# A perceiver block on one core: an attention product computed in the first step, layer norms beside the batches, a rearranged last batch

## The chip, the core and the metric

The kernel runs on one core of a Trainium2 chip. The core has TensorE (PE; its weight loads are shown as PEld), VectorE (DVE), ScalarE (ACT), GpSimd (POOL) and SyncE (SP), each with its own queue of instructions that it works through in order. DMAs are issued by SP, ACT and POOL. The metric is the device time of one execution in microseconds (us), the median over several executions. One execution is also profiled; its span runs from the first to the last instruction.

## What is computed

Eight batches of 128 rows with 512 columns go through three residual blocks. Normalisation is over the columns.

```python
x = x + xattn(layernorm(x), ctx)   # 8 heads of 64, softmax over 2048 context rows
x = x + attn(layernorm(x))         # n = layernorm(x); adds n + read
#   queries = n@Wq+bq, keys = n@Wk+bk, values = n@Wv+bv; causal mask;
#   probs = softmax(logits, axis=1) / sqrt(512), read = probs @ values
x = x + ffn(layernorm(x))
#   h = relu(n@w1.T + b1); rounded to a float of 4 exponent and 3 mantissa bits,
#   as is w2; out = h@w2.T + b2, rounded to 5 exponent and 10 mantissa bits
```

The context has 2048 rows of 384 columns in each batch, so its keys and values (`pk`, `pv`) are most of the work.

## The kernel before

**Cross-attention.** The loop over batches `b` has four steps `m`, one for each pair of heads. A step issues `scores(b, m)` (TensorE `sc`; VectorE copies each bank to `p` and takes maxima, L530), then `attend` of the pair before (TensorE `po`, L571), then one *unit* of other TensorE work, and around it `exps` for the two heads (ScalarE, L544), `turns` (VectorE transposes `p` in 32 by 32 blocks, L557, and SP issues 16 DMAs that put the blocks into `pT`, L560). `pT` and `p` have one buffer each. The unit is `v_proj(b, 1)`, `v_proj(b+1, 0)` or `k_proj(b+1, m-2)`: products of blocks of the context in a scheme with 20 products instead of 24, whose operands are sums of context blocks (`sum_half`, on POOL except for batch 0) and of weight blocks (`sum_w`). A unit is a generator: its first part runs between the two `exps` (`first_of`), the rest after `turns` (`all_of`).

**Order.** Under `manual_schedule` an engine keeps the order of the program text; otherwise a scheduler orders its instructions. TensorE keeps the text's order to the end. ScalarE (`in_turn`) and VectorE (`first`) keep it until these two contexts are closed, in the last batch at the end of step 0. POOL and SP are always left to the scheduler. All queues are worked off in order on the chip.

**Start.** Before the loop, batch 0 is prepared: `k_plain`, the queries of all batches (`q_norm`, `q_turn`, `q_proj`; normed rows of the second half in the buffer `v0`), `sum_half` of both halves on VectorE, `keep_rows` (POOL adds the output bias `bo` to all rows, L503, and SP stores them to `xd`), and preparation for the self-attention. There, logits are computed as n (Wk Wq^T) n^T with side terms: `weight_by_bias` multiplies each weight by a bias row (`dot`, L303), `turn_weight` transposes both weights in blocks on VectorE (L313), and `keep_weights` stores them by 32 DMAs (L320) in DRAM.

**Rows.** `normalized_first` and `normalized` (in step 0 of the next batch) divide by the softmax sums, `project` (L609, L612) adds the output projection to the rows of the batch before, and SP stores these to `xr` (L614). `bring_rows` loads all rows back in the last batch.

**Last batch, self-attention, ffn.** In step 0 of batch 7 `enter_self_attention` closes the pools of the context and loads weights through POOL's queue. `SelfAttention` 0 has rows 0 to 3, 1 has rows 4 to 7. The last batch's units are, in step 1, `both_weights` (product of the two weights, `psw`, L664) followed by `norm` and `turn` of rows 0 to 3; in step 2 `keys` (`psk`, L678); in step 3 `weights` of four rows (`pl`, L693, mask, softmax). Then come the `values` (`psv`, L717), `attend` of the last pair, `project` of batch 7, norms and turns of rows 4 to 7, the second half of the self-attention, `read` (`pr`, L725), and the ffn: `hidden` (`ph`, L927; ScalarE's relu, L931; `quantize`, five VectorE instructions, L40 to L44), `output` (`pf`, L936) and `finish`.

Of the kernel before, what the change touches and what calls it, by code (L numbers as in the profile page):

```python
# [23 lines left out]
E4M3 = (3, -6, 8)  # L24
# [3 lines left out]
def quantize(nc, pool, out, x, fmt, tag):  # L28
# [15 lines left out]
    nc.vector.tensor_scalar(out, r, 2.0 ** (128 - over), 2.0 ** (over - 128), ALU.mult, ALU.mult)  # L44


@with_exitstack
def tile_perceiver_block(
# [226 lines left out]
    bo = tmp.tile([P, D], F32, tag="t", name="bo")  # L275
    nc.sync.dma_start(bo, xa_bo.partition_broadcast(P))
# [3 lines left out]
    side = const.tile([P, 2, NK], F32, tag="side", name="side")  # L280
    both_biases = const.tile([P, 1], F32, tag="both_biases", name="both_biases")
    turned_w = [dram.tile([D, D], F32, tag=f"tw{i}", name=f"tw_{i}") for i in range(2)]

    def across(v, n, name):

        line = dram.tile([1, D], F32, tag=f"line{n}", name=f"line_{n}")
        nc.gpsimd.dma_start(line.rearrange("o (k p) -> p (o k)", p=P), v)
        return line[0].partition_broadcast(P)

    for i, a in enumerate((sa_wq, sa_wk)):  # L290
        nc.sync.dma_start(w_sa[:, i], a.rearrange("(k p) n -> p k n", p=P))
    bias_rows = []
    for n, a in (("bk", sa_bk), ("bq", sa_bq)):
        c = const.tile([P, NK], F32, tag=f"c{n}", name=f"c_{n}")
        nc.gpsimd.dma_start(c, a)
        t = tmp.tile([P, D], F32, tag="t", name=f"row_{n}")
        nc.gpsimd.dma_start(t, across(c, n, n))
        bias_rows.append(t)

    unread = ps_acc.tile([P, D], F32, tag="po", name="unread")  # L300

    def dot(to, one, two):
        nc.vector.scalar_tensor_tensor(unread, one, 1.0, two, ALU.mult, ALU.mult, accum_out=to)  # L303

    def weight_by_bias(i):

        for k in range(NK):
            dot(side[:, i, k : k + 1], w_sa[:, i, k], bias_rows[i])

    def turn_weight(i, ks):  # L310

        for k in ks:
            nc.vector.transpose(w_sa[:, i, k], w_sa[:, i, k])  # L313

    def keep_weights():
        for i in range(2):
            for k in range(NK):
                for a in range(Q):
                    to = turned_w[i][:, k * P + a * SQ : k * P + (a + 1) * SQ]
                    nc.sync.dma_start(  # L320
                        to.rearrange("(g i) j -> i g j", i=SQ),
                        w_sa[ts(a, SQ), i, k].rearrange("p (g j) -> p g j", j=SQ),
                    )
# [177 lines left out]
    def keep_rows(g):  # L501
        for b in range(g * GB, (g + 1) * GB):
            nc.gpsimd.tensor_tensor(xs[b], xs[b], bo, ALU.add)  # L503
        nc.sync.dma_start(xd[:, ts(g, GB), :], x_in[:, ts(g, GB), :])
# [96 lines left out]

    def load_x(b):
        xs[b] = xp.tile([P, D], F32, tag="x", name=f"x_{b}")
        nc.sync.dma_start(xs[b], xd[:, b, :])

    def project(b, ot):
# [6 lines left out]
        if b < B - 2:  # L613
            nc.sync.dma_start(xr[:, b, :], xs[b])  # L614

    def bring_rows():
        t = keep.tile([P, B, D], F32, tag="keep", name="rows")
        nc.gpsimd.dma_start(t[:, : B - 2], xr[:, : B - 2])
        nc.gpsimd.dma_start(t[:, B - 2 :], xd[:, B - 2 :])
        for r in range(B):  # L620
            xs[r] = t[:, r, :]


    def load_row(pool, src, name):
        t = pool.tile([P, D], F32, tag=name, name=name)
        nc.gpsimd.dma_start(t, src.partition_broadcast(P))
# [7 lines left out]
    class SelfAttention:  # L634


        def __init__(self, g, pool, w):
            self.g, self.pool = g, pool
            self.swq, self.swk, self.swv, self.u, self.bv, self.mask = w
            self.c = {}  # L640
# [17 lines left out]
        def both_weights(self):  # L658

            self.both = self.pool.tile([P, NK, D], F32, tag="sq", name="both")  # L660
            for m in range(NK):
# [7 lines left out]
                if m == 1:  # L669
                    yield  # L670
# [358 lines left out]
```

## Time and profile before

| | |
|---|---|
| median of 3 executions | 1127.91 us (1126.43 to 1130.67) |
| profiled execution | 1124.47 us, span 1122.7 us |
| granted TensorE clock, mean | 0.992 |
| TensorE busy in the span | 1098.4 us (98%) |
| VectorE, ScalarE, POOL busy | 844.1, 334.7, 236.1 us (75%, 30%, 21%) |
| one of the batches 1 to 6 | 102.86 us (scores at 227.97, 330.84, ...) |
| scores of batch 7 to the first `ph` | 157.84 us (816.72 to 974.56) |
| first `ph` to the end of the chain's last piece of `ph` | 126.1 us (974.56 to 1100.65) |
| from there to the end | 22 us |

A matrix product of float32 is recorded as two matmul entries. TensorE's busy time is modelled from pipelined entries, so 98% does not mean that it runs at its peak. A name such as `pv_z` is a tile of the program with its buffer number left out. In the pieces of the chain the columns are start and duration in us, then engine, tile, line and number of instructions. In the stretches in order of time they are start, duration, engine, line, operation, tiles and shapes, number, and in brackets the idle time of the engine just before, with what ended it.

### The profile page before, as it was taken

How to read it: one execution, taken by the hardware profiler on the slowest of the kernel's cores; microseconds unless marked ns; L12 is line 12 of the kernel's file. 1: busy time of each engine (PE TensorE's matmuls, PEld its weight loads, DVE VectorE, ACT ScalarE, POOL GpSimd, SP SyncE). 2: the span in 40 equal slices, each digit the busy share in tenths (PEclk: the TensorE clock that was granted, in tenths of full speed). 3: DMA queues.
4: the chain of work that ended last, by engine and by line, in shares of the span. 5: the costliest groups of instructions: out<-in, count | busy, mean ns of one | idle time of the engine just before them, and what ended most of it. 6: DMA issues, size and time to landing. Idle time of an engine off the chain costs nothing.

```text
span 1122.7 us, 16820 instructions
## 1 busy us (share of the span) xinstructions
PE 1098.4 (98%) x6254; PEld 830.2 (74%) x6254; DVE 844.1 (75%) x1760; ACT 334.7 (30%) x527; POOL 236.1 (21%) x328
## 2 busy tenths in 40 slices
PE   9989999999999999999999999999998999999997
PEld 4467788877878887888778788878874564687775
DVE  3988767767867786677777667866787468997777
ACT  3323232222223332322222233323232323232221
POOL 1401610440053045004400530350002100000001
PEclk9989999999999999999999999999998999999999
DMA  8858544553553355445535533554474445200001
GB/s 213 279 129 135 129 99 111 146 151 76 142 143 83 85 148 146 101 109 146 150 76 142 141 76 85 148 137 92 108 209 120 108 95 225 75 1 20 10 10 38
DMA packets 66785, 130.10 MB, mean 116 GB/s; under 512 B 27456, under 2 KB 32592, under 8 KB 65808
## 3 DMA queue, kind: packets, MB, share of 16 engines
q1 hardware_dynamic: 64144, 121.68, 43.6%
q0 software_dynamic: 1696, 6.57, 2.0%
q8 instruction: 49, 0.80, 0.3%
q10 hardware_dynamic: 864, 0.79, 0.2%
q14 instruction: 32, 0.26, 0.1%
HBM read 51.92 MB, written 9.97 MB: 55 GB/s over the span
## 4 chain that ended last, share of the span: by engine, by line
PE 88%; DVE 7%; DMA 3%; issue 1%; ACT 0%; SPq 0%; ACTq 0%; DVEq 0%
PE pv_z L450 20%; PE pk_z L427 19%; PE po L571 11%; PE sc L526 10%; PE ph L927 9%; PE pv_b L450 3%; PE pk_b L427 3%; PE psk L678 2%; PE psv L717 2%; PE py L609 2%; PE pf L936 2%; DMA x<-in_ctx_t_dram 1%; PE psw L664 1%; DVE m L205 1%; DMA x_in<-in_x_dram 1%; DVE x L205 1%
## 5 line engine op out<-in xcount | busy, mean ns | idle before, releaser
L544 ACT ACTIVATE p<-p,nm 128x2048 f32<-128x2048 f32 x64 | 128.2, 2003 | 429.4 <-DVE nm L538 291.2
L557 DVE STREAM_TRANSPOSE p<-p 128x512 f32<-128x512 f32 x256 | 158.9, 680 | 82.8 <-ACT p L544 82.6
L530 DVE TENSOR_SCALAR_CACHE_REDUCE p<-sc 128x512 f32<-128x512 f32 x256 | 159.0, 686 | 21.0 <-PE sc L526 18.6
L450 PE MATMUL pv_z<-wv_sums,x 128*128 128x256 f32 x640 | 158.0, 381 | 1.8 <-DVE v L353 1.8
L427 PE MATMUL pk_z<-x,wk_sums 128*128 128x256 f32 x600 | 151.0, 385 | 5.5 <-DVE kt L353 4.9
L205 POOL TENSOR_TENSOR m<-x 128x256 f32<-128x256 f32 x70 | 51.1, 731 | 485.4 <-DMA x<-in_ctx_t_dram 388.9
L450 PEld LDWEIGHTS pv_z<-wv_sums,x 128*128 128x128 f32 x640 | 120.4, 190 | 20.3 <-DVE v L353 2.2
L427 PEld LDWEIGHTS pk_z<-x,wk_sums 128*128 128x128 f32 x600 | 113.4, 191 | 25.1 <-DVE kt L353 5.6
L571 PEld LDWEIGHTS po<-pT,v 128*64 128x64 f32 x2048 | 112.4, 138 | 25.0 <-issue 23.5
L526 PE MATMUL sc<-kt,q 64*128 64x512 f32 x512 | 120.9, 604 | 3.8 <-DVE p L530 2.5
L571 PE MATMUL po<-pT,v 128*64 128x128 f32 x2048 | 120.2, 276 | 0.0
L927 PE MATMUL ph<-xf,w 128*128 128x256 f32 x512 | 111.3, 379 | 0.0
L450 PE MATMUL pv_z<-wv_sums,m 128*128 128x256 f32 x448 | 107.5, 380 | 0.2 <-ACT v L347 0.2
L927 PEld LDWEIGHTS ph<-xf,w 128*128 128x128 f32 x512 | 97.2, 190 | 13.9 <-issue 0.5
L427 PE MATMUL pk_z<-m,wk_sums 128*128 128x256 f32 x420 | 102.0, 381 | 0.0
L526 PEld LDWEIGHTS sc<-kt,q 64*128 64x128 f32 x512 | 47.6, 187 | 63.7 <-issue 52.7
L450 PEld LDWEIGHTS pv_z<-wv_sums,m 128*128 128x128 f32 x448 | 83.3, 190 | 13.3 <-issue 0.9
L427 PEld LDWEIGHTS pk_z<-m,wk_sums 128*128 128x128 f32 x420 | 79.8, 191 | 11.7
L347 ACT COPY v<-pv_z 128x512 f32<-128x512 f32 x112 | 62.8, 588 | 59.8 <-PE pv_z L450 59.6
L347 ACT COPY kt<-pk_z 128x512 f32<-128x512 f32 (+1 forms) x112 | 59.7, 558 | 63.1 <-PE pk_z L427 62.7
L205 POOL TENSOR_TENSOR x<-x 128x256 f32<-128x256 f32 x98 | 69.9, 730 | 0.8 <-DMA x<-in_ctx_t_dram 0.7
L350 DVE TENSOR_TENSOR v<-pv_z,v 128x512 f32<-128x512 f32 x96 | 63.2, 686 | 5.1 <-PE pv_z L450 5.0
(187 smaller groups left out, 1233.1 us busy)
## 6 DMA issues: line engine op xcount, KB each, us to landing
pT<-p SPq DMA_DIRECT2D x512, 128.0 KB, 2.4
x<-in_ctx_t_dram SPq DMA_DIRECT2D x45, 512.0 KB, 5.6
w<-in_w_t_dram SPq DMA_DIRECT2D x1, 4096.0 KB, 12.6
w2f<-in_w_t_dram SPq DMA_DIRECT2D x16, 256.0 KB, 2.7
x_in<-in_x_dram SPq DMA_DIRECT2D x8, 256.0 KB, 13.0
xd<-x_in SPq DMA_DIRECT2D x2, 1024.0 KB, 4.4
qd<-xq SPq DMA_DIRECT2D x8, 256.0 KB, 5.2
q<-qd SPq DMA_DIRECT2D x8, 256.0 KB, 3.1
```

Source lines behind the costliest of these rows:

```text
L205: eng.tensor_tensor(x_block(b, h, to), x_block(b, h, one), x_block(b, h, two), ALU.add if op == "+" else ALU.subtract,)
L347: nc.scalar.copy(outs[ij], views(ps))
L350: nc.vector.tensor_tensor(outs[to], views(ps), outs[other], op)
L427: nc.tensor.matmul(ps[:, ts(i, BK)], wk_sums[:, WSLOT[WAT[r]], f2, :], x_block(b, h, XAT[r]), start=start and i == 0, stop=True, skip_grou ...
L450: nc.tensor.matmul(ps[:, ts(t, 256)], x[:, ts(t, P)], wv_sums[:, WSLOT[WAT[r]], :], start=start and t == 0, stop=True, skip_group_check=True,)
L526: nc.tensor.matmul(pair[i], q[r, :], kts[b, m // 2][r, m % 2, ts(n, 512)], start=True, stop=True)
L530: nc.vector.tensor_scalar(p[:, :, i].rearrange("p g (t i) -> p t g i", i=SQ)[:, ts(n, Q)], pair[i].rearrange("p (t g i) -> p t g i", g=Q, ...
L544: nc.scalar.activation(p[:, :, i], p[:, :, i], AF.Exp, bias=nms[b, m][:, i : i + 1], scale=SCALE, accum_out=sums[b][:, h : h + 1],)
L557: nc.vector.transpose(p[:, g, i], p[:, g, i])
L571: nc.tensor.matmul(pos[b][h * DH : (h + 1) * DH, ts(m, P)].rearrange("p (a i) -> p a i", a=Q), v[:, jt % 8, ts(2 * m + h, DH)], turned_[b, ...
L609: nc.tensor.matmul(ps, ot[:, ts(k, P)], wo[:, k, :], start=(k == 0), stop=(k == NK - 1))
L927: nc.tensor.matmul(ps[:, :n], w1[:, k, ts(c, P)], xt[:, k, at], start=(k == 0), stop=(k == NK - 1),)
```

## The change

1. The product of the two self-attention weights moves from step 1 of the last batch to step 0 of batch 0. The transposed weights stay in SBUF (`turned_w`, in buffer `v0`) instead of DRAM, and the product goes to `both_w` in DRAM.
2. The bias rows are spread by a VectorE transpose and small DMAs between the two `sum_half` of batch 0; `bo` is loaded by POOL into a buffer that they leave, and `keep_rows` comes after them, with its stores on POOL's queue.
3. For rows 0 to 5 the self-attention's norm is done in the loop, for batch `b-1` in steps 1 and 2 of batch `b` (`row_stats`, `row_scale`, `norm_rows`); the transposed normed rows go to `xtd` in DRAM. Loads and stores of rows move from SP's queue to ScalarE's.
4. In the last batch the units are `keys`, `weights` with two `values`, and two `values`; ScalarE and VectorE keep the text's order to the end of the loop. What follows is reordered.
5. Rounding to 4+3 bits takes four VectorE instructions and a second ScalarE pass over the PSUM bank, scaled by 2^20 and rounded to bf16 by its output type.

```diff
+def round_e4m3(nc, pool, out, x, c, tag):
+    d = pool.tile(list(x.shape), F32, tag=f"{tag}_d", name=f"{tag}_d")
+    nc.vector.tensor_scalar(c, c, LOWEST, HIGHEST, ALU.max, ALU.min)
+    nc.vector.tensor_tensor(d, c, x, ALU.subtract)
+    nc.vector.tensor_tensor(out, c, d, ALU.subtract)
+    nc.vector.tensor_scalar(out, out, INFINITE, 1.0 / INFINITE, ALU.mult, ALU.mult)
...
     for i, a in enumerate((sa_wq, sa_wk)):
         nc.sync.dma_start(w_sa[:, i], a.rearrange("(k p) n -> p k n", p=P))
+    nc.gpsimd.memset(squares, 0.0)
+    for n, a in enumerate((sa_bk, sa_bq)):
+        nc.sync.dma_start(squares[:, n, :NK], a)
+    def across(n):
+        line = dram.tile([NK, P], F32, tag=f"line{n}", name=f"line_{n}")
+        nc.vector.transpose(squares[:, n], squares[:, n])
+        for a in range(Q):
+            nc.gpsimd.dma_start(line[:, ts(a, SQ)], squares[a * SQ : a * SQ + NK, n])
+        return line.rearrange("k p -> (k p)").partition_broadcast(P)
...
+    def both_weights():
+        tq, tk = (turned_w[0][:, i].rearrange("p (k m) c -> p k m c", m=NK) for i in range(2))
+        for n in range(NK):
+            ps = bank(f"pw_{n}")
+            for m in range(NK):
+                nc.tensor.matmul(
+                    ps, tk[:, n, m], tq[:, :, m], start=(m == 0), stop=(m == NK - 1)
+                )
+            t = xp.tile([P, D], F32, tag="x", name=f"both_{n}")
+            nc.scalar.copy(t, ps)
+            nc.scalar.dma_start(both_w[:, n], t)
...
+    def row_scale(b):
+        sd = small.tile([P, 1], F32, tag="sd", name=f"sd_s_{b}", bufs=4)
+        nc.scalar.activation(sd, stats[b][:, 1:2], AF.Sqrt, bias=eps)
+        nc.scalar.activation(warm, eps, AF.Exp)
+        u = tmp.tile([P, D], F32, tag="t", name=f"u_{b}")
+        nc.scalar.dma_start(u, u_line)
+    def norm_rows(b):
...
+        nc.vector.reciprocal(rs, sd)
+        nc.vector.tensor_scalar(xn, xs[b], mv[:, 0:1], rs, ALU.subtract, ALU.mult)
+        pt = bank(f"pt_s_{b}")
+        row_constant(b, xn, u, pt)
+        nc.vector.tensor_tensor(xs[b], xs[b], xn, ALU.add)
+        for k in range(NK):
+            nc.tensor.transpose(pt[:, ts(k, P)], xn[:, ts(k, P)], ident)
+        xt = tmp.tile([P, NK, S], F32, tag="t", name=f"xt_s_{b}")
+        nc.scalar.copy(xt, pt.rearrange("p (k t) -> p k t", k=NK))
+        nc.scalar.dma_start(xtd[:, :, ts(b, S)], xt)
...
     sum_half(0, 1, nc.vector)
+    spread_biases()
     sum_half(0, 0, nc.vector)
...
-    for g in range(NG):
-        keep_rows(g)
     load_q(0)
     dot(both_biases, bias_rows[0], bias_rows[1])
     weight_by_bias(0)
+    bo = tmp.tile([P, D], F32, tag="t", name="bo")
+    nc.gpsimd.dma_start(bo, xa_bo.partition_broadcast(P))
+    for g in range(NG):
+        keep_rows(g)
+    turn_weight(0)
     all_of(k_proj(0, 0, (1,)))
...
             elif m == 1:
-                unit = sa0.both_weights()
+                unit = sa0.keys()
             elif m == 2:
-                unit = sa0.keys(sa0.both)
-            else:
                 for r in sa0.rows:
                     sa0.weights(r)
+                unit = sa0.some_values(sa0.rows[:2])
+            else:
+                unit = sa0.some_values(sa0.rows[2:])
...
             exps(b, m, 1)
+            if b == m == 0:
+                all_of(both_weights())
...
+            if m == 1 and b > 0 and not last:
+                row_stats(b - 1)
+            if m == 2 and b > 0 and not last:
+                norm_rows(b - 1)
             turns(b, m)
...
             if unit:
                 all_of(unit)
+            if m == 1 and b > 0 and not last:
+                row_scale(b - 1)
+            if m == 2 and b > 0 and not last:
+                nc.scalar.dma_start(xr[:, b - 1, :], xs[b - 1])
+            if m == 2 and b < B - 2:
+                load_x(b)
+            if m == 2 and last:
+                bring_rows()
...
-                    first.close()
-                    in_turn.close()
-                    sap, w = enter_self_attention()
-                    sa0 = SelfAttention(0, sap, w)
-            if last and m == 1:
-                for r in sa0.rows:
-                    sa0.norm(r)
-                    sa0.turn(r)
+                    sap, w, sa0 = enter_self_attention()
+    first.close()
+    in_turn.close()
     for r in sa0.rows:
-        sa0.values(r)
+        sa0.read(r)
     sa1 = SelfAttention(1, sap, w)
-    for r in sa1.rows[:-1]:
-        sa1.norm(r)
+    sa1.norm(B - 2)
     attend(B - 1, NK - 1)
     ot = normalized(B - 1, normalized_first(B - 1))
-    for r in sa0.rows[:2]:
-        sa0.read(r)
+    sa1.turn(B - 2)
+    for r in sa1.rows[:2]:
+        sa1.values(r)
     xa.close()
     project(B - 1, ot)
-    sa1.norm(sa1.rows[-1])
-    for r in sa1.rows[:-1]:
-        sa1.turn(r)
-    for r in sa0.rows[2:]:
-        sa0.read(r)
-    sa1.turn(sa1.rows[-1])
+    sa1.norm(B - 1)
+    sa1.values(B - 2)
+    sa1.turn(B - 1)
```

## The prediction

> **What bounds the kernel now.** I read the chain of waits by engine first, then what TensorE itself waited for, then the pieces of the chain in order of time, and last the single stretches where the chain leaves TensorE.
>
> ```profile
> PE 88%; DVE 7%; DMA 3%; issue 1%; ACT 0%; SPq 0%; ACTq 0%; DVEq 0%
> ```
> ```profile
> PE pk_z L427 <- DVE kt L353: 4.9, 1, 4.9
> PE sc L526 <- DVE p L530: 2.5, 1, 2.5
> ...
> PE pv_z L450 <- DVE v L353: 1.8, 1, 1.8
> PE pt_s L131 <- DVE xn_s L118: 1.8, 1, 1.8
> PE sc L526 <- DVE rows L612: 1.3, 1, 1.3
> ```
> The chain is TensorE for 88% of the span, and TensorE's waits (total, times, longest) are single events. From 227.97 us to 831 us it never pauses: six batches of 102.86 us. So a cost in the middle counts only if TensorE has to do it or is made to wait; VectorE and ScalarE have room there. The losses lie at the two ends. At the start, TensorE stands 4.93 us before 67.90 and loses 2.05 us in the second `v_proj` (19.33 us from 105.78 to 125.11 for 80 products of 216 ns, 17.28 us). At the end, from the first scores of the last batch (S = 816.72) to the first `ph` (974.56) are 157.84 us. Adding up the TensorE pieces of the chain there (sc, po, pv, rb, py, psw, pt_s, psk, pl, psv, pr, pt_f) gives 146.8 us, so 11 us are lost, around 836-853 and 931-938. The last stretch, from 1100.65, is VectorE's.
>
> ```profile
> 860.50 13.93 PE psw L664 x32
> ...
> 883.46 13.93 PE psk L678 x32
> ...
> 904.67 3.77 PE pl L693 x32
> 908.44 13.73 PE psv L717 x32
> 922.17 3.65 PE po L571 x64
> ```
> The reader is to see that between two `po` pieces of the last batch (attention of one head pair) there lies a long product: psw, psk, psv, 14 us each. They cover the road of the probabilities from scores to `po`, read from the last step:
>
> ```profile
> 903.94 2.00 ACT L544 ACTIVATE p<-p,nm 128x2048 f32<-128x2048 f32 x1 [5.83 <-DVE nm L538]
> 905.94 1.99 ACT L544 ACTIVATE p<-p,nm 128x2048 f32<-128x2048 f32 x1
> ```
> ```profile
> 906.07 4.87 DVE L557 STREAM_TRANSPOSE p<-p 128x512 f32<-128x512 f32 x8 [2.21 <-ACT p L544]
> ```
> ```profile
> 909.23 10.04 SPq L560 DMA_DIRECT2D pT<-p  x16
> ```
> Scores start at 897.39; VectorE has emptied them at 903.86; two exponentials of 2.1 us each; transposes of 0.61 us, the first four beside the second exponential; 16 DMAs in 10.04 us, the last issued at 918.7 and landed 2.4 us later, 921.1. That is **24 us** from scores to the earliest `po`, or 12.8 us from the end of the second exponential. TensorE came at 922.17, only 1 us later: this cover is nearly used up already.
>
> **The product of the two weights (L664 to the first step).** Its 16 products leave the last batch (13.93 us) and run in batch 0, step 0, between the second exponential and the rest of `v_proj(0,1)`. TensorE is busy there, so it is +13.93 us early. Its operands come by 32 DMAs as before; the last would be issued near 92-95 us (16 DMAs of about 0.63 us after the second turn at about 84), TensorE asks at about 105: no wait. The four copies and four ACT-queue stores lie beside the products.
>
> **Bias rows and `bo`.** Before, `bo` was added by POOL beside VectorE's sums:
>
> ```profile
> 38.16 0.42 DVE L205 TENSOR_TENSOR m<-x,m 128x256 f32<-128x256 f32 x1
> 38.62 1.37 DVE L205 TENSOR_TENSOR x<-x 128x256 f32<-128x256 f32 x1
> ```
> ```profile
> 38.16 11.41 POOL L503 TENSOR_TENSOR x_in<-x_in,bo 128x512 f32<-128x512 f32 x8 [19.88 <-DVE m L205]
> ```
> One VectorE subtraction of 0.42 us takes 1.37 while POOL adds; eight of them cost 8 us, on the chain. The move frees these 8 us. But VectorE then comes to `dot` at about 55, and it needs two rows that now wait for a transposition in the middle of the sums, eight small POOL DMAs and two broadcasts. The small loads of `squares` are issued behind 2 MB of `w_sa`, which landed 12.7 us after its issue at 31.3, so at 44-45; eight POOL issues of 0.55 us; a small landing, estimated at 3 us below the 5.3 us row of `c_bk` because there are 16 pieces for a row instead of 128; a broadcast of 6.0 us (row_bq). That puts the rows at 59-61. Five dots (0.79 each) and the four transposes that now precede `k_proj` (2.45) end at 65.5-67.4, against 67.43 before. **I take 0**; bounds are -4.9 (the whole wait goes) and +5 (rows at 66).
>
> The additions of `bo` go to about 73-84 us, beside `weight_by_bias(1)`. Here a rule speaks against the move. The row is a VectorE multiplication with two SBUF inputs (L649): 0.69 us alone, 1.77 us at 936.44 beside a POOL addition at 936.40. The Trainium skill, SBUF — State Buffer, section "Who interferes with whom", says why: VectorE with two SBUF inputs and a POOL instruction that reads SBUF exclude each other for the whole instruction. By the row and the rule the four dots cost 4 x 1.1 = 4.4 us more; by a reading in which only plain additions suffer, nothing. I take 4.4, but VectorE has four transposes less in that stretch (2.45) and TensorE ran about 4 us ahead of need there: 0 on the chain. In return POOL's sums for batch 1 fall beside the weight product, so the 3.16 us that one L384 took at 118.70 under POOL goes: **-2.05**.
>
> **Layer norms beside the batches (rows 0 to 5).** Each batch gets four transposes on TensorE, 0.44 us: +2.62 in six batches, taken from the end. VectorE: statistics 0.85 us in step 1; in step 2 reciprocal 0.15, xn 0.55, dot 0.78, 0.15, sum 0.69 = 2.3 us. Both stand where VectorE waits for ScalarE anyway:
>
> ```profile
> 672.87 2.49 DVE L557 STREAM_TRANSPOSE p<-p 128x512 f32<-128x512 f32 x4 [2.21 <-ACT p L544]
> ```
> The bracket is an idle time of 2.21 us: hidden, and the transposes are ready when TensorE comes 9 us into the step. ScalarE's two table loads (1.28 each), the square root and most of its DMA issues come after the unit, where it idles 13.70 us before the next exponential. One is not covered: copy and store of `xt` stand ahead of three evacuations. The same place in step 0 has a copy (rb) without a store, and there TensorE arrives 0.4 us after the bank it needs is read. A DMA issue takes 0.45 (ACT's median) to 0.58 us, and TensorE itself comes 0.44 later only for both: between 0 and 0.7, **I take 0.5 x 6 = +3**. SP loses twelve DMAs; it waited for nobody that TensorE waited for: 0.
>
> **The last batch.** TensorE sheds 13.93 + 2.62 = 16.55 us. But VectorE and ScalarE now keep the written order through this batch; before, they were free from its step 1. I follow it from S, each step as above:
> - Scores of step 1 start at S+28.4 (unchanged). The unit is `keys`; ScalarE must evacuate its first two blocks before the second exponential. The second block ends on TensorE at 3.63+3.65+6.96 = 14.2 after the scores, evacuation 0.7, exponential 2.1, then 12.6: `po` may start 29.65 after, TensorE is there at 24.85. **Wait 4.8.**
> - Step 2: the weights of rows 0-3 need `keys`, and TensorE reaches them behind this `po`. Their four exponentials (1.57 us apart; 911.39 to 912.70 and on for one row) stand ahead of both big ones: 3.65+0.94, then 6.0 to the last small exponential, 4.2, 13 = 27.8 after the previous `po`; TensorE has 17.95 of work (po, pl, two psv, sc). **Wait 9.9.**
> - Step 3: VectorE must add bias to values of row 2, which TensorE makes only after that `po`, before it may transpose: 3.65+3.45+0.65+3.1+11.9 = 22.8; TensorE has 14 (po, two psv, four pr). **Wait 8.8.**
>
> The last `po` starts at S+108.7 instead of S+105.45. Behind it the order is better: with three psv inside the gap that `project` and the last norm leave, I get 20.5 us to `psk` and 26.6 (psk 13.93, 0.75, pl, one psv, pt_f, pr) to `ph`: S+155.8. So the stage gains **2.0**, not the 16.55 it sheds.
>
> **Rounding.** Until 1100 TensorE covers it and ScalarE's second pass (0.47 per chunk of 1.73): 0, and the 0.5 us wait of pf goes. At the end one block of 512 counts: now 0.42+0.42+0.69+0.69+0.43 = 2.65. New by the nearest row (L44, bf16 written from f32, 0.43): 0.43+0.69+0.69+0.43 = 2.24. By VectorE: DVE Perf Modes, "The perf-mode tier table", a scalar operation with bf16 on both sides runs at four per cycle, which I estimate as half of 0.42: 1.8. No row here shows it; I take the rule, 0.85, less what the second activation delays: **-0.8**, -1.3 with pf.
>
> **Sum.** 13.93+2.62+3+0-2.05-2.0-1.3 = +14.2 us. On the profiled execution, 1124.47 (span 1122.7 and 1.8 around it): 1138.7. The median shown is 3.4 higher, 1127.91: **1142**.
>
> **Rivals.** (1) *The waits of the last batch stay hidden* (chance 0.18): the probabilities arrive before TensorE, as in every step before. Then the stage is 130.3 of work and 3 of waits, 24.5 less; with the start gaining 4.9 and ScalarE 1 instead of 3, the sum is -15: 1113. For it: no `po` waited before, and the start has 8 us of holes. Against: 24 us of road and units now of 7 us. It decides from where the last `po` starts before S+95. (2) *Late bias rows* (0.10): if POOL's first broadcast sits in its queue ahead of the second row's small DMAs, these go out only when the first have landed (c_bq cost such a wait of 8.77): rows at 75, +14: 1156. (3) *It cancels* (0.08): start at its best (-4.9), stores free (-3), last batch 6 us shorter: 1128. The sum itself has 0.64, with a range of its own of 1133 to 1152.
>
> About 0.5% (5.6 us) is what a measurement of this kernel can tell from no change. Faster 0.19, same 0.10, slower 0.71. The range 1124 to 1156 leaves out most of rival 1.
>
> **What would show it.** A TensorE wait before the last three `po`, of about 5, 10 and 9 us; the second exponential of step 1 behind two `sk`; steps of batches 1-6 at 103.8 us instead of 102.86; `pw` at 105-120 us without holes; `dot` waiting for the row's DMA near 60. Wrong, if the `po` wait under 2 us each, or if batches grow by more than 2 us.

## The result, and the profile after

The changed kernel takes 1156.45 us (1155.68 to 1157.45, 4 runs), the kernel before 1127.45 us in the same session: a ratio of 1.0253, 95% interval 1.0229 to 1.0276. The forecast was 1142, with a range of 1124 to 1156: the direction was right, the size was half, and the time lies just above the upper end of the range. The profiled execution has a span of 1153.9 us, 31.2 more than before, and a mean granted clock of 0.980 instead of 0.992.

Cutting both profiles at the same instructions shows where the 31.2 us arise (times from the first rows of `sc` and `ph`):

| stretch | before | after | difference | predicted |
|---|---|---|---|---|
| start to scores(0, 0) | 92.25 | 83.69 | -8.56 | 0 |
| to scores(0, 1) | 32.79 | 44.81 | +12.02 | +11.88 |
| to scores(7, 0) | 691.61 | 701.90 | +10.29 | +5.62 |
| S to the first `ph` | 157.75 | 175.72 | +17.97 | -2.0 |
| to the end | 148.30 | 147.78 | -0.52 | -1.3 |

Only the second row is right in size. TensorE's waits after (total, times, longest) name most of the rest:

```profile
PE po L609 <- DMA pT<-p: 21.2, 3, 8.1
PE sc L564 <- DVE p L568: 5.8, 1, 5.8
PE pk_z L465 <- ACT kt L385: 3.3, 7, 0.6
...
PE sc L564 <- DVE sv L782: 1.4, 1, 1.4
PE pr L791 <- DVE sv L782: 1.2, 1, 1.2
```

The forecast waits before the last three `po` are there, 21.2 us against 23.5. The second line was not forecast: one wait of 5.8 us in step 1 of the last batch. The third is TensorE waiting until ScalarE has copied keys (`kt`) out of a bank: about half a microsecond in each of the batches 1 to 6, and 0.56 us in batch 0, which the kernel before has too. The wait of 5.8 us, in order of time (start, duration, engine, line, operation; in brackets the idle time before and what ended it):

```profile
858.27 0.55 POOL L707 DMA_DIRECT2D u<-line  x1
...
866.64 0.69 DVE L682 SCALAR_TENSOR_TENSOR unread<-xn_s,u 128x512 bf16<-128x512 f32 x1 [4.76 <-DMA u<-line]
...
867.80 0.69 DVE L568 TENSOR_SCALAR_CACHE_REDUCE p<-sc 128x512 f32<-128x512 f32 x1 [0.27 <-issue]
...
868.55 2.07 PE L564 MATMUL sc<-kt,q 64*128 64x512 f32 x2 [5.83 <-DVE p L568]
```

`unread` is the output of the row constant of row 6, which `sa1.norm(6)` computes. In the text it stands behind the loop, after `first` and `in_turn` are closed. The scheduler may place it where it likes, and placed it ahead of the score copies of step 1. There it waits for the row `u`, a late load in POOL's queue, and the copies that free TensorE's banks wait behind it.

And TensorE itself was slow where it came out of a wait. First the four `po` of the last batch after this, in order of time; then three of these stretches in the table of windows (length, busy time of PE, PEld, DVE, ACT and POOL with their counts, granted clock, DMA share, GB/s):

```profile
870.55 4.81 PE L609 MATMUL po<-pT,v 128*64 128x128 f32 x64
...
898.11 6.36 PE L609 MATMUL po<-pT,v 128*64 128x128 f32 x64 [5.18 <-DMA pT<-p]
...
929.24 6.16 PE L609 MATMUL po<-pT,v 128*64 128x128 f32 x64 [7.99 <-DMA pT<-p]
...
955.41 5.04 PE L609 MATMUL po<-pT,v 128*64 128x128 f32 x64 [8.07 <-DMA pT<-p]
```
```profile
898.11:904.47 6.36, 6.36 (x65) 6.19 (x65) 0.00 (x0) 0.00 (x0) 0.00 (x0) 0.57 0.00 0
929.24:935.40 6.16, 6.16 (x65) 5.99 (x65) 0.00 (x0) 0.00 (x0) 1.35 (x3) 0.59 0.15 44
955.41:960.50 5.09, 5.09 (x65) 4.92 (x66) 0.00 (x0) 0.00 (x0) 0.00 (x0) 0.73 0.00 0
```

The same 64 products take 3.71 us elsewhere. The excess of the four is 7.5 us (22.37 less 4 x 3.71), and the prediction has no term for it. The kernel before has one such `po` in its last batch, behind two waits for the scores, an excess of 1.3 us:

```profile
855.48 5.02 PE L571 MATMUL po<-pT,v 128*64 128x128 f32 x64
```

At the start, the order of the changed kernel pays more than was granted to it:

```profile
35.80 4.33 POOL L313 DMA_DIRECT2D line<-squares  x8 [34.39 <-DVE squares L311]
...
41.67 0.55 POOL L321 DMA_DIRECT2D row<-line  x1 [0.98 <-DMA line<-squares]
```
```profile
50.20 0.69 DVE L325 SCALAR_TENSOR_TENSOR unread<-row,row 128x512 f32<-128x512 f32 x1
```

The small DMAs that spread the bias rows go out at 35.8, and VectorE multiplies with the rows at 50.2 without a wait, where the prediction had them landing at 59 to 61. The weight product stands in step 0 as forecast, as long as forecast and without a hole; it comes at 97.4 us instead of about 105 because the whole start is shorter:

```profile
97.41 13.90 PE L354 MATMUL pw<-turned_w 128*128 128x512 f32 x32
```

### The profile page after: what moved, and what is told of

The parts are those of the page before. It is cut to its first block, busy times and chain, and to the rows that moved or that the text cites. A ratio compares the mean times of both kernels' runs of the same rounds, so it can differ in the third digit from the quotient of the medians.

```text
span 1153.9 us, 16960 instructions
## 1 busy us (share of the span) xinstructions
PE 1109.3 (96%) x6250; PEld 836.8 (73%) x6254; DVE 811.1 (70%) x1736; ACT 383.6 (33%) x625; POOL 231.4 (20%) x334
## 5 line engine op out<-in xcount | busy, mean ns | idle before, releaser
L609 PEld LDWEIGHTS po<-pT,v 128*64 128x64 f32 x2048 | 118.7, 144 | 46.6 <-issue 45.1
L609 PE MATMUL po<-pT,v 128*64 128x128 f32 x2048 | 126.4, 284 | 21.2 <-DMA pT<-p 21.2
L564 PE MATMUL sc<-kt,q 64*128 64x512 f32 x512 | 125.2, 606 | 7.2 <-DVE p L568 5.8
L1004 PEld LDWEIGHTS ph<-xf,w 128*128 128x128 f32 x512 | 97.2, 190 | 13.9 <-issue 0.5
L564 PEld LDWEIGHTS sc<-kt,q 64*128 64x128 f32 x512 | 50.0, 187 | 69.4 <-issue 53.2
```

Of the source, the lines that this page charges most:

```text
L564: nc.tensor.matmul(pair[i], q[r, :], kts[b, m // 2][r, m % 2, ts(n, 512)], start=True, stop=True)
L609: nc.tensor.matmul(pos[b][h * DH : (h + 1) * DH, ts(m, P)].rearrange("p (a i) -> p a i", a=Q), v[:, jt % 8, ts(2 * m + h, DH)], turned_[b, ...
L1004: nc.tensor.matmul(ps[:, :n], w1[:, k, ts(c, P)], xt[:, k, at], start=(k == 0), stop=(k == NK - 1),)
```

## The experiments

Ratios are to the kernel before, which ran on the same chip in each session. The changed kernel stands at 1.0253. "The last stage" is scores(7, 0) to the first `ph`: 157.75 before, 175.72 after.

**e1: the norm of row 6 stays at its place.**

```diff
-    first.close()
-    in_turn.close()
     for r in sa0.rows:
         sa0.read(r)
     sa1 = SelfAttention(1, sap, w)
     sa1.norm(B - 2)
+    first.close()
+    in_turn.close()
     attend(B - 1, NK - 1)
```

> Only change against the changed kernel: VectorE and ScalarE keep the text's order until behind sa1.norm(6), so that the norm of row 6 can no longer be drawn into steps 0 and 1 of the last batch. Theory (the drawn-in norm is what lengthens step 1: VectorE waits 4.76 us for its row constant's load, TensorE 5.8 us before p in step 1, then a slower po and a table load of 1.28 us): the 5.8 us wait of sc goes, scores of batch 7 to first ph fall from 175.9 to about 168 us, the whole by 6 to 9 us, to 1148-1150. Rival (the road of the probabilities is what sets the last batch, and the hoist only filled idle time): the wait of sc goes but the po waits grow by as much; the whole stays within 2 us of 1156.

Measured: 1145.0 us, ratio 1.0181 (1.0158 to 1.0204), 0.7% or 8 us below the changed kernel; the last stage takes 164.66 us, 11.1 less. The wait of `sc` is gone, and TensorE's waits for pT grew by only 2.5 us:

```profile
PE po L609 <- DMA pT<-p: 23.7, 3, 10.3
```

So the drawn-in norm cost some 11 us of this profile, and the rival falls. The 11 are more than its wait of 5.8: the `po` behind it was slow (4.81 us), ScalarE had to load its exponential's table again (1.28 us, on the path), and the later `po` were slower too.

**e2: a free order in the last batch.** VectorE and ScalarE are released at the end of step 0, as in the kernel before; units and TensorE's order stay. The second edit, `u` first in the text, had no effect: POOL's order is the scheduler's, and it issued `u` at 858.94, as late as before.

```diff
+        u_first = load_row(wsa, u_line, "u")
...
                 if last:
+                    first.close()
+                    in_turn.close()
                     sap, w, sa0 = enter_self_attention()
-    first.close()
-    in_turn.close()
```

> Against the changed kernel: the text's order for VectorE and ScalarE ends at step 0 of the last batch, as in the kernel before, and the load of the self-attention's row constant is put first in POOL's queue. Units and TensorE's order stay those of the changed kernel. Theory A (my prediction's: the units are too short for the 24 us from scores to po): a free order can only take out what stands ahead of the exponentials, so the three po waits of 5.2, 8.0, 8.1 us stay at 3 or more each, and scores to first ph stays over 160 us (before: 157.8); whole 1142-1152. Rival B (the written order alone makes the waits): the three po waits sink under 1.5 us each, scores to first ph under 150 us, whole under 1135.

Measured: 1132.84 us, ratio 1.0063 (1.0041 to 1.0086); the last stage takes 152.17 us, although the 5.3 us wait for `u` remains. Neither expectation holds as it stands: of three waits for pT one vanished, two stayed.

```profile
894.10 3.71 PE L609 MATMUL po<-pT,v 128*64 128x128 f32 x64
...
914.61 3.71 PE L609 MATMUL po<-pT,v 128*64 128x128 f32 x64 [2.53 <-DMA pT<-p]
...
932.80 5.38 PE L609 MATMUL po<-pT,v 128*64 128x128 f32 x64 [3.98 <-DMA pT<-p]
```

The reason stands in ScalarE's rows of step 1. First the changed kernel, then e2:

```profile
874.54 2.00 ACT L582 ACTIVATE p<-p,nm 128x2048 f32<-128x2048 f32 x1
...
879.09 0.69 ACT L746 ACTIVATE sk<-psk,side 128x512 f32<-128x512 f32 x1 [2.46 <-PE psk L742]
882.47 0.69 ACT L746 ACTIVATE sk<-psk,side 128x512 f32<-128x512 f32 x1 [2.69 <-PE psk L742]
883.05 1.99 ACT L582 ACTIVATE p<-p,nm 128x2048 f32<-128x2048 f32 x1
```
```profile
874.69 2.00 ACT L582 ACTIVATE p<-p,nm 128x2048 f32<-128x2048 f32 x1
...
876.69 1.99 ACT L582 ACTIVATE p<-p,nm 128x2048 f32<-128x2048 f32 x1
```

In the written order the second exponential stands behind two evacuations of keys that TensorE has yet to make: 8.5 us from exponential to exponential, 2.0 in the free order. With nothing ahead of the exponentials the road from scores to `po` is the 24 us that the prediction read: scores of step 3 start at 908.38, `po` at 932.80, 24.4 later. What remains, 2.5 and 4.0 us, is the road against units that are too short. So the written order makes about 15 us of the 21 us of waits, and the units that are too short to cover the road make 6.5.

**e3: longer units in the last batch.**

```diff
             elif m == 1:
-                unit = sa0.keys()
+                unit = sa0.some_values(sa0.rows)
             elif m == 2:
-                for r in sa0.rows:
-                    sa0.weights(r)
-                unit = sa0.some_values(sa0.rows[:2])
-            else:
-                unit = sa0.some_values(sa0.rows[2:])
+                unit = sa0.keys()
...
-                if unit:
+                if unit and not (last and m > 0):
                     first_of(unit)
...
             if m == NK - 1:
                 inverse_sums(b)
+                if last:
+                    for r in sa0.rows:
+                        sa0.weights(r)
...
             if m == 2 and last:
                 bring_rows()
+                sa1 = SelfAttention(1, sap, w)
+                sa1.norm(B - 2)
+                nc.scalar.activation(warm, eps, AF.Exp)
+                sa1.turn(B - 2)
-    first.close()
-    in_turn.close()
+    for r in sa1.rows[:2]:
+        sa1.values(r)
     for r in sa0.rows:
         sa0.read(r)
-    sa1 = SelfAttention(1, sap, w)
-    sa1.norm(B - 2)
+    rs_last = normalized_first(B - 1)
+    first.close()
+    in_turn.close()
     attend(B - 1, NK - 1)
-    ot = normalized(B - 1, normalized_first(B - 1))
-    sa1.turn(B - 2)
-    for r in sa1.rows[:2]:
-        sa1.values(r)
+    ot = normalized(B - 1, rs_last)
+    xf0 = normed_rows(0, "xt0")
...
```

> Against the changed kernel: in the last batch alone other units lie between two po. Step 1 has the values of all four rows (14 us), step 2 the keys (14 us), step 3 the weights of the four rows; in steps 1 to 3 the unit stands whole behind the transposes and none of it before the second exponential; the norm and turn of row 6 are done at the end of step 2, and two values of rows 4 and 5 and the four reads come before the last attend. The norm of rows 0 to 3 of the ffn's input is drawn before project. Theory A (cover): with 14 us units and nothing ahead of the exponentials the po waits fall from 5.2, 8.0, 8.1 to under 3 each, scores of batch 7 to first ph from 175.9 to 135-145, whole 1115-1125, under the kernel before. Rival (the slow TensorE clock and loads in the last batch set the time, not the cover): the waits fall, but the stage stays over 155 us; whole 1136 or more.

Measured: 1121.38 us, ratio 0.9965 (0.9952 to 0.9977); the last stage takes 141.45 us, 34.3 less than in the changed kernel and 16.3 less than before. That is about the 16.55 us of work that TensorE sheds there. One wait for pT is left, and the `po` are fast but for the one behind it:

```profile
910.63 3.71 PE L609 MATMUL po<-pT,v 128*64 128x128 f32 x64
...
931.18 5.38 PE L609 MATMUL po<-pT,v 128*64 128x128 f32 x64 [2.26 <-DMA pT<-p]
```

The theory holds and the rival falls. With these units the written order is no hindrance, since nothing that TensorE has yet to compute stands ahead of an exponential. e3 changes several things at once, the units, their place behind the exponentials, the norm of row 6 and the reads, and the runs do not divide its gain among them.

**e12: TensorE kept busy in its waits.** On e1, products that nobody reads stand ahead of the last three `po`.

```diff
+    def keep_busy(n, m):
+        ps = bank(f"fill_{m}")
+        for i in range(n):
+            nc.tensor.matmul(ps, ident, wo[:, i % NK, :], start=True, stop=True)
...
             if m > 0:
+                if last and m > 1:
+                    keep_busy((11, 18)[m - 2], m)
                 attend(b, m - 1)
...
+    keep_busy(22, 4)
     attend(B - 1, NK - 1)
```

> The kernel of e1 (the norm of row 6 in its place), and TensorE is given products whose result nobody reads (11, 18 and 22 of identity by a weight block, about 0.43 us each) where it otherwise waits 5.1, 8.3 and 10.3 us for pT before the last three po. Theory (after a wait TensorE runs slower for some us: the 64 products of a po took 5.1, 5.5 and 5.5 us there, 3.7 elsewhere): the three waits shrink to under 1 us each, the three po take 3.7 us, and the products behind them are as fast as in the kernel before, so that the whole is 4 to 7 us below e1 although TensorE does 22 us more work. Rival (the po are slow because the parts of pT arrive one by one, or because of memory traffic): the po stay over 5 us each, the whole is within 1 us of e1 or longer.

Measured: 1161.0 us, ratio 1.0296 (1.0264 to 1.0328), longer than e1, because I took one of the two entries of a float32 product for the whole: a filling product costs 0.87 us, and the fills last 9.71, 17.16 (in part at a clock of 0.50) and 19.05 us, together 22.2 more than the waits that they replace. The stage grew by only 17.0. The difference is in the `po`. First e1's windows, then e12's, with columns as above:

```profile
889.39:894.47 5.08, 5.08 (x65) 4.91 (x65) 0.00 (x0) 0.00 (x0) 0.00 (x0) 0.72 0.00 0
919.27:924.76 5.49, 5.49 (x65) 5.32 (x65) 0.00 (x0) 0.71 (x1) 0.00 (x0) 0.66 0.00 0
946.54:952.05 5.51, 5.51 (x65) 5.34 (x66) 0.00 (x0) 0.00 (x0) 0.00 (x0) 0.66 0.00 0
```
```profile
893.58:897.30 3.72, 3.72 (x66) 3.55 (x65) 0.00 (x0) 0.00 (x0) 0.00 (x0) 1.00 0.02 4
931.06:934.80 3.74, 3.74 (x66) 3.57 (x65) 0.00 (x0) 0.00 (x0) 0.00 (x0) 1.00 0.00 0
965.04:968.80 3.76, 3.76 (x66) 3.59 (x66) 0.00 (x0) 0.00 (x0) 0.00 (x0) 1.00 0.00 0
```

Full clock and 3.7 us each: 4.95 us back for three, 22.2 - 4.95 = 17.3 against the 17.0 measured. So each of these waits for pT, of 5.1 to 10.3 us in the changed kernel and in e1, cost its own length and 1.3 to 2.7 us more behind it. Since the fills ran past the arrival of pT, these runs alone don't exclude that pieces of pT coming in one by one also slow a `po`; the clock column accounts for the whole excess without it. That fills of the right length would gain 5 us was not tried.

**e6: `bo` added beside VectorE's sums again.**

```diff
+    bo = tmp.tile([P, D], F32, tag="t", name="bo")
+    nc.sync.dma_start(bo, xa_bo.partition_broadcast(P))
     w_sa = vp.tile([P, 2, NK, D], F32, tag="v1", name="w_sa")
...
+    for g in range(NG):
+        keep_rows(g)
     spread_biases()
...
-    bo = tmp.tile([P, D], F32, tag="t", name="bo")
-    nc.gpsimd.dma_start(bo, xa_bo.partition_broadcast(P))
-    for g in range(NG):
-        keep_rows(g)
     turn_weight(0)
```

> Against the changed kernel: the output bias is loaded at its old place and POOL adds it to the rows ahead of the bias rows' spreading, so beside VectorE's sums of context halves as in the kernel before; everything else as in the changed kernel. Theory (the gain of 8.6 us at the start comes from the eight POOL additions that no longer lengthen VectorE's subtractions): the first scores come 5 to 8 us later than in the changed kernel (83.7), at 89-92, and the whole is 4 to 8 us longer, 1160-1164. Rival (the gain comes from the transposes moved behind k_proj's operands and from an earlier start of TensorE's clock): first scores within 2 us of 83.7, whole within 2 us of 1156.

Measured: 1160.75 us, ratio 1.0319 (1.0292 to 1.0346), a span 4.9 us longer than the changed kernel's. Scores(0, 0) come at 88.61, 4.9 later, and TensorE waits again for VectorE:

```profile
65.14 0.88 PE L467 MATMUL pk_z<-x,wk_sums 128*128 128x256 f32 x2 [2.90 <-DVE kt L393]
...
88.61 1.98 PE L566 MATMUL sc<-kt,q 64*128 64x512 f32 x7
```

From 60 us to the scores the clock was 0.94 here, 0.89 before and 1.00 in the changed kernel from 57 on. So 4.9 of the 8.56 us hang on `bo`'s place: with it go VectorE's long subtractions, a wait of TensorE, and the slow clock behind the wait. Of the other 3.7, the wait and the clock explain most: before, the wait was 4.93 us instead of e6's 2.90, the clock was lower, and a first wait of TensorE at the very start was 1 us longer. The rest was not taken apart.

**e7: the rounding of before.** The five VectorE instructions instead of the four and ScalarE's second pass.

```diff
-            up = tp.tile([P, D], BF16, tag="w2c", name=f"w2c_{c}")
-            nc.scalar.activation(up, w, AF.Abs, scale=UP)
-            round_e4m3(nc, tp, w2[:, c, :], w, up, "qw")
+            quantize(nc, tp, w2[:, c, :], w, E4M3, "qb")
...
-            round_e4m3(nc, tp, firsts[b0][:, c0 : c0 + per, :], h, up, "qh")
+            quantize(nc, tp, firsts[b0][:, c0 : c0 + per, :], h, E4M3, "qh")
```

> Against the changed kernel: the rounding to 4+3 bits is the one of the kernel before (five VectorE instructions, one ScalarE pass over the bank). Theory: first ph to the end is 0.5 to 1.3 us longer (147.6 to about 148.5), but ScalarE's key copies of rows 4 to 7 no longer stand behind its Abs pass over a weight chunk, which waits for VectorE's rounding: psk 14.0 instead of 15.7 us, and scores of batch 7 to first ph 1.5 to 2.5 us shorter; the whole within 1.5 us of 1156, more likely below. Rival (the four instructions are worth what they save): the whole 1 to 3 us longer.

Measured: 1170.03 us, ratio 1.0376 (1.0351 to 1.0401), 13.9 us more than the changed kernel. Both expectations fall. `psk` does take 14.00 us instead of 15.70, but what goes before it came 2.0 later, and the last stage is unchanged (175.91). Nor is the 15.70 the rounding's: `psk` takes 14.00 us also in e4 and e5 below, which keep the new rounding, and the clock during it was 0.89 in the changed kernel and 1.00 in e4. The loss is behind it, 162.0 us from `ph` to the end instead of 147.8:

```profile
1043.87 1.09 PE L152 MATMUL pt_f<-ident,xn_f 128*128 128x128 f32 x4 [9.65 <-DVE xn_f L139]
```

VectorE is at the rounding and comes too late to the norm of rows 4 to 7. The last of the 16 blocks of w2 was rounded 19.8 us after the first `ph` here, 12.8 after it in the kernel before and 11.5 after it in the changed kernel. TensorE's waits behind `ph` add up to 11.0 us, where the changed kernel has none, and the clock behind the longest was 0.50 for some 6 us. The changed kernel's order leaves VectorE less time ahead of the ffn, and only the shorter rounding (1.97 us for a block of 512 of the hidden layer, 2.65 before) makes that order affordable. Part 5, which I priced at -1.3, is worth 14 us where part 4 stands; in the balance against the kernel before, these only make good what the new order would have lost.

**e4, e5: the growth of the batches.** e4 leaves out the load of `u` in the batches and takes part of another weight in its place; e5 moves the store to `xtd` behind the unit.

```diff
-        u = tmp.tile([P, D], F32, tag="t", name=f"u_{b}")
-        nc.scalar.dma_start(u, u_line)
-        stats[b] = stats[b], sd, u
+        stats[b] = stats[b], sd, wo[:, 0, :]
```
```diff
-        nc.scalar.dma_start(xtd[:, :, ts(b, S)], xt)
+        stats[b] = xt
...
             if m == 2 and b > 0 and not last:
+                nc.scalar.dma_start(xtd[:, :, ts(b - 1, S)], stats[b - 1])
                 nc.scalar.dma_start(xr[:, b - 1, :], xs[b - 1])
```

> Against the changed kernel: the 256 KB broadcast of the row u that each of the batches 1 to 6 loads on ScalarE's queue in step 1 is left out; the row constant of rows 0 to 5 is taken with a part of another weight in place of u, so the logits of those rows differ. The last batch is untouched. Theory (this load delays the 16 DMAs that fill pT in step 1 and 2, and so VectorE's first copy of the next scores): batches 1 to 6 lose 0.3 to 0.9 us each of the 10.3 us that they grew by, the whole falls by 2 to 5 us, and SP's wait at the pT DMAs of step 1 (3.8 us) goes. Rival (the growth is the transposes, 0.44, and the evacuations behind the store of xt, 0.5, alone): within 1 us of the changed kernel, 1154-1157 on its scale.

> Against the changed kernel: only the issue of the store of the transposed normed rows (to xtd, ACT queue, 0.55 us) moves from step 2's start, ahead of three evacuations, to behind the unit. Theory: the 3.3 us that TensorE waits for ACT's kt in seven places fall to about 0.5, batches 1 to 6 grow by 7.3 instead of 10.3 us, the whole is 2.5 to 3.5 us shorter. Rival (the copy of xt alone is enough to be late, the issue is hidden): less than 1 us.

Measured: e4 1153.7 us, ratio 1.0231 (1.0206 to 1.0255); scores(0, 1) to scores(7, 0) grow by 7.96 us instead of 10.29. The intervals of e4 and of the changed kernel overlap, so it is the profiles that tell. Step 2 of batch 4, first in the changed kernel, then in e4:

```profile
569.91 4.32 PE L564 MATMUL sc<-kt,q 64*128 64x512 f32 x16
...
572.36 0.69 DVE L568 TENSOR_SCALAR_CACHE_REDUCE p<-sc 128x512 f32<-128x512 f32 x1 [1.65 <-DMA pT<-p]
```
```profile
569.36 3.70 PE L564 MATMUL sc<-kt,q 64*128 64x512 f32 x16
```

The load of `u` goes out at 562.26 in the changed kernel. The last nine `pT` DMAs of this fill, issued beside and behind it, land after 4.4 to 4.8 us, all 16 of e4 after 2.3 to 2.4. VectorE can't copy the next scores into `p` before they have landed, so the scores take longer. In the batches 1 to 6 of the changed kernel six scores are stretched like this, by 3.4 us together; in e4 two are, by 1.2, and in the kernel before none. That is e4's 2.3 us.

e5 takes 1160.71 us, ratio 1.0290 (1.0263 to 1.0316); its batches grow by 14.33. In e5 TensorE's waits for ACT's `kt` fall from 3.3 to 0.6 us, as the theory said, and still it loses: its stretched scores add up to 10.4 us. The worst is in batch 4:

```profile
590.20 0.56 ACTq L926 DMA_DIRECT2D xtd<-xt_s  x1
590.79 0.74 ACTq L927 DMA_DIRECT2D xr<-x  x1
591.57 0.73 ACTq L646 DMA_DIRECT2D x<-xd  x1
...
602.83 0.69 DVE L568 TENSOR_SCALAR_CACHE_REDUCE p<-sc 128x512 f32<-128x512 f32 x1 [4.18 <-DMA pT<-p]
...
603.59 1.28 PE L564 MATMUL sc<-kt,q 64*128 64x512 f32 x2 [2.03 <-DVE p L568]
...
604.79 5.18 PE L609 MATMUL po<-pT,v 128*64 128x128 f32 x64
```

Three row DMAs go out within 2 us beside the 16 that fill `pT`. The six `pT` DMAs issued next take 4.1 to 6.6 us to land, where the first of the 16 took 2.3, and the last four go out only from 598.43 on; `p` has one buffer, so VectorE can't copy the next scores into it; TensorE's banks stay full for 2.0 us; and the `po` behind that wait is slow, 5.18 us. A row DMA that nobody waits for costs TensorE time through a buffer. Why batch 4 is hit hardest, here and in e8, is not shown.

**e8 to e11: both on the longer units.** e8 is e3 with e5's edit. e9 keeps `u` rounded to bf16, loaded once in batch 0. e10 issues the store in step 3 instead, and e11 does both:

```diff
+            if m == 3 and b > 0 and not last:
+                nc.scalar.dma_start(xtd[:, :, ts(b - 1, S)], stats[b - 1])
```

> The kernel with the longer units in the last batch (e3) together with the store behind the unit (e5). Theory (the two lie in different stages and add): 2.5 to 3.5 us below e3, at a ratio of 0.993-0.995 to the kernel before. Rival (what TensorE gains in the middle it waits for at the next copy of scores): the same as e3, 0.996-0.997.

> The kernel with the longer units (e3), with one more edit: the row u is loaded once, in batch 0, and kept rounded to bf16, so that the batches 1 to 6 and the last batch no longer load it (the row constants then use the rounded row). Theory (e4 showed 2.3 us, from a load that collides with the fill of pT): batches 1 to 6 grow by about 8 us instead of 10.3, the whole is 2 to 3 us below e3, a ratio to the kernel before of 0.994 to 0.995. Rival (in e4 other data, not the load, made the difference): as e3, 0.9965.

> The kernel with the longer units (e3), with one more edit: the store of the transposed normed rows is issued one step later, in step 3 behind the second exponential, so neither ahead of evacuations that follow a copy nor beside the two other row DMAs at the end of step 2. Theory (e5 lost because three row DMAs together delayed the last pT of step 2): TensorE's waits for ACT's kt fall from 3.3 to under 1 us and no wait of sc for p appears in batches 1 to 6; they grow by 7 to 8 us instead of 10.3; the whole is 2 to 3 us below e3. Rival (any place costs as much as it saves): same as e3 within 1 us.

> The longer units (e3) with both edits, the row u kept as bf16 and the store in step 3. Theory (both lie in steps 1 to 3 of the batches and add): 4 to 5.5 us below e3, a ratio to the kernel before of 0.9915 to 0.993; batches 1 to 6 grow by 5 us. Rival: 0.9945 or more, because what is left of the growth is the transposes and pT as such.

| | ratio to before | interval | kt waits, us | growth of the batches, us |
|---|---|---|---|---|
| e3 | 0.9965 | 0.9952 to 0.9977 | 3.3 | 9.25 |
| e8 | 0.9963 | 0.9951 to 0.9975 | 0.6 | 11.04 |
| e9 | 0.9950 | 0.9939 to 0.9961 | 3.3 | 10.50 |
| e10 | 0.9945 | 0.9929 to 0.9961 | 0.6 | 7.80 |
| e11 | 0.9936 | 0.9912 to 0.9959 | 0.6 | 6.19 |

e3's batches are the changed kernel's word for word and grow by 9.25 in place of 10.29, so two profiles can differ by 1 us here. For e8 the rival holds: what the waits for `kt` give, stretched scores take (8.5 us, 2.4 in e3). e10's place for the store is as good as its theory said in waits, but the gain over e3 is not certain from the intervals. e9's ratio lies at the edge of what its theory said, and its profile shows why the batches gain so little. As in e4 and e11, no scores of step 2 are stretched in batches 1 to 6, where every version with the load has 1.5 to 2.8 us of it; so it is the load that stretches them. But the one load left in batch 0 stretches scores there by 1.6 us, and the profiled execution was 3.4 us longer than e9's median. e11 falls between its theory and its rival; it has the lowest ratio of the versions run: 1118.46 us, 0.6% below the kernel before and 3.1% below the changed one (0.9936 / 1.0253 = 0.969), but its interval overlaps that of e10.

## Why the prediction was right in direction and short in size

The miss of 17 us is smaller than its parts. By luck the start was 8.6 us shorter than forecast; the other terms together were 26 us too low.

- **Weight product, and the stall under POOL:** right. 13.90 us without holes, and with the stall gone +12.02 for +11.88.
- **Bias rows and `bo`:** the step that failed is the landing of the small loads: they were put behind the 2 MB of `w_sa`, issued at 31.3 and landed at 44 to 45 us. In the changed kernel `w_sa` goes out at 18.5 and 19.2, the small loads have landed at 32.1, their transposition is over by 35.8, and the spread rows land at 43.8 and 45.9. So the rows never held up the dots, and the whole wait went, as the lower bound of -4.9 had it. Below that bound lie the clock that TensorE no longer loses behind the wait and about 1 us of an earlier start. Of the 4.4 us for four dots beside POOL, 1.6 were paid: the additions came earlier than I had them (58 to 68.6 us), and only the first dot, 2.29 us, met them; the next three took 0.70.
- **Layer norms beside the batches:** +10.29 for +5.62. The evacuations behind `xt`'s store were priced right (3.0; six of the seven waits, 2.7 us, lie in these batches). Priced at nothing were ScalarE's DMAs: their traffic beside the pT fill. The prediction counted their issues on their queue and not what they do to the transfers on other queues. e4, e5 and e9 show the mechanism, and the stretched scores are 3.4 of the remaining 4.7 us; the last 1.3 are not taken apart.
- **The last batch:** the waits of `po` were right, 5.2, 8.0 and 8.1 for 4.8, 9.9 and 8.8, and so was their cause, what stands ahead of the exponentials (e2, e3). The stage was 20 us off, 16 of them because of two things. The step "VectorE and ScalarE now keep the written order through this batch" was taken to hold for what is executed in the batch; what follows the closing lines is free and was drawn into it (e1, 11.1 us). And every wait was priced at its own length, without the slow clock behind it (e12, 4.95 us for three of them). Two short waits of e1 for values (1.4 and 0.7 us) are in no term of the prediction either; the remaining 2 us are not taken apart.
- **Rounding:** -0.52 for -1.3. A block of 512 took 1.97 us on VectorE where I had 1.8: the scalar operations on bf16 took 0.29 us each, not 0.21, the half of 0.42. On blocks of 1024 they took 0.43, so about 0.15 us of each does not grow with the block (an estimate from these two). That the old rounding would have cost 14 us in the new order was not seen.
- **Rivals:** the first (waits stay hidden) is refuted as the changed kernel stands, and e3 shows what it takes to make it true. The second has the measured time to the microsecond and the wrong cause: the bias rows were early. The third did not occur.

The slow clock is in the Trainium skill, TensorE: Matmul & The Clock Gate, Part 1: after an idle window of about 3.4 us the array runs at half rate until it has been busy for such a window, and the windows are free-running, they do not start with the work. As an estimate from the page, a wait can cost up to 3.4 us behind it, half of the rest of a slow window and of the whole next one. The traces agree in kind. Here are three windows of the changed kernel around the `po` at 898.11, with columns as above:

```profile
896.74:900.15 3.41, 2.04 (x20) 2.07 (x22) 0.00 (x0) 0.00 (x0) 0.00 (x0) 0.50 0.12 25
900.15:903.57 3.42, 3.42 (x36) 3.42 (x34) 0.00 (x0) 0.00 (x0) 0.00 (x0) 0.50 0.00 0
903.57:906.98 3.41, 3.41 (x39) 3.24 (x36) 0.71 (x3) 0.49 (x2) 0.00 (x0) 1.00 0.02 5
```

The first 5.46 us of this `po` ran at half rate, which is the 2.7 us that it lost. In every profile the slow stretches inside the program last one to four times 3.41 us and begin on one grid of 3.41 us. So the price of a wait depends in part on where it falls in the grid: e4 has the last batch of the changed kernel word for word and waits of nearly the same length, and its four `po` took 5.84, 5.22, 5.69 and 6.61 us. A slow window can follow one that was not idle throughout. The wait of 2.26 us in e3 lay inside one window, and the next was slow; the wait of 2.53 us in e2 lay across two, and none was. Yet a wait of 1.39 us in e12 was followed by a slow window too, so how much idle time it takes is not settled here.

## What to carry to other kernels

Price a new TensorE wait at its own length and then count what runs behind it at the clock that the profile shows after such waits; a row of the same products after an earlier wait (5.02 us for 64 `po` at 855.48 before, 3.71 elsewhere) gives a first size beforehand. Where two orders meet, a written one and a scheduler's, look at what follows the seam: it may be moved ahead of it, and wait there in front of the critical work. And put no instruction that depends on TensorE's next unit ahead of the work that TensorE will wait for: with nearly the same work, other units and places for the norms and reads turned +2.5% into -0.35% (e3).

## What the runs showed of the hardware that was not expected

- In the changed kernel and in e1 the granted clock of the 64 products behind a wait for pT was 0.57 to 0.73, and 1.00 when the waits were filled with products nobody reads; the `po` took 5.0 to 6.4 us and 3.7 us. The slow clock came in whole stretches of 3.41 us, on one grid in each execution.
- One DMA of 256 KB on ScalarE's queue raised the time to landing of the `pT` DMAs (128 KB each, on SP's queue) from 2.3 to 2.4 us to 4.4 to 4.8; three such DMAs within 2 us raised it to 4.1 to 6.6 and delayed VectorE's next write to their source buffer by 4.18 us in one batch of e5.
- Of the schedule rather than the hardware: an engine order that is written by hand and then released did not only leave later instructions free: a norm behind the release was executed in steps 0 and 1 of the last batch, ahead of the score copies, and cost 11 us there.
